# Later chains of squarings: one product and VectorE transposes per step, and the steps dealt out anew

## The chip, the cores and the metric

The kernel runs on one core of a Trainium2 chip. The metric is the device time of one execution in microseconds (us), the median of several runs. TensorE (PE) multiplies matrices, VectorE (DVE), ScalarE (ACT) and GpSimd (POOL) do the element-wise work, and SyncE (SP) issues most DMAs.

## The reference

Four layers are applied to x of 8 batches, 512 channels and 32 x 32 places. The change lies in layer 0, whose core is

```
z = jnp.einsum('bcn,bcm->bnm', f_x, g_x)
S = jnp.linalg.svd(z, compute_uv=False)
sigma = S[:, 0][:, None, None]
attn = z / sigma
z2 = jnp.einsum('bnm,bcm->bcn', attn, h_x).reshape(b, MID, h, w)
return conv1x1(z2, Wv, bv) + x
```

with 64 channels in the middle (MID). Layer 1 is attention over the 1024 places with softmax, with group normalization ahead of it; layer 2 is a second attention with 128 channels; layer 3 is a convolution with the signs of its weights and of its input. Each adds its input. Layers 1 to 3 carry most of the arithmetic.

## The kernel before

**Sigma without a decomposition.** The largest singular value of z squared is the largest eigenvalue of F G, where F and G are the 64 x 64 Gram matrices of f and g. The kernel squares this product again and again and takes traces on the way; sigma comes from the logarithms of the traces. Two batches make a pair: their 64 x 64 matrices stand as two diagonal blocks in a 128 x 128 tile (zero elsewhere), so one matmul squares both. There are four pairs. `gm[j]` holds F, G and the product H of h and g for pair j, each 128 x 128, masked by `mask2` where `gram` (L1337 to L1352) evicts them.

**A chain** (`chain`, from L1016) is the work of one pair: a generator that yields after each of its 22 steps. A matmul gives lhsT transposed times rhs, so squaring a matrix takes its transpose as the stationary operand. The kernel before carries both: `products` (L1026) makes the square (L1029) and the square of the transpose (L1030), each 128 x 128 x 128, and `evict` copies both to SBUF as `cur`, of 128 x 256. Every third step is scaled by the trace of before: a matmul of one column with `mask2` adds up the diagonal (`total`, L1060), VectorE copies it (L1061), takes the reciprocal (L1083) and scales the eviction (L1051). The other two steps are evicted by ScalarE (L1043); on the second of them VectorE takes the diagonal from PSUM (L1056) for the next trace. One chain has 21 steps with a product and 8 totals. The last step writes the scaled H over F (L1112), and `weights0` uses it for the batch.

**The stages.** In an opening, layer 0's projections of all batches, the grams and the weights' products are made. The chain of the first pair in `order` (batches 6 and 7) runs here, with an order of PE's instructions written out by hand, among fillers; it is `chain(jl, True)`, whose two products go to two PSUM banks. The other three chains (`behind`, `chain(j, False)`) run later, between the big products of the batches. The main part has 8 PSUM banks of 128 x 512. It begins with `make_u` for the first batch; then `fast` runs once for each batch: layer 1's scores (`scores1`, 28 yields), v (`make_v`, 14), the values' product (`values1`, 14), layer 2's projections (`project2`), layer 2's scores (`scores2`, 8 tiles) together with the next batch's `make_u`, layer 2's values, and layer 3 (`leave`). The big products follow a scheme of seven products in place of eight (`seven`, matmuls at L388), with evictions by ScalarE, VectorE and GpSimd; values' products stand at L557.

**Where chain steps stand.** `next(behind)` does one step. In `make_u` one is done at every second yield. In `fast` the function `chore(2)` does one at each second call: in `scores1`, where `rest3` (the rest of layer 3 of the batch before) is done and some yields are left out, in `make_v` and in `values1`. There are 66 steps, and in the profile the last product is at 717 us, in the third batch. `entering` (for the batch after the present one) calls the chain's steps at once where its pair is not ready yet. The framework's scheduler then orders the instructions of each engine, so an engine's order can differ somewhat from the program's.

**What hangs on layer 2's sums.** `inverse_sums` (L829 to L838 and on) adds up the exponentials by a matmul, takes the reciprocal on VectorE (L838), writes it to DRAM and reads it back spread over all partitions by DMA (`rfull`); the values are scaled with it (`att`, L967) ahead of the matmuls of `close2` (L675).

Of the kernel before, what the change touches and what calls it, by code (L numbers as in the profile page):

```python
# [16 lines left out]
P = 128  # L17
# [68 lines left out]
def kernel(  # L86
# [96 lines left out]
        return t.rearrange("p g j -> p (g j)")  # L183

    mask2 = block_ones(MID, 1.0, "mask2")
    gmat = block_ones(GROUP, 1.0 / GROUP, "gmat")

    fold = a1.tile([P, 2, MID], F32, tag="fold", name="fold")
# [54 lines left out]

    r_dram = [dram.tile([4, N // 4], F32, name=f"r_dram{i}") for i in range(2 * B)]
    f_dram = [dram.tile([P, HF], F32, name=f"f_dram{b}") for b in range(B)]
    gm = [keep.tile([P, 3, P], F32, tag=f"gm{j}", name=f"gm{j}") for j in range(NPAIR)]
    sw3 = wpool.tile([P, CC, C // 2], F16, tag="sw3", name="sw3")
    round3 = const.tile([P, 1], F32, tag="round3", name="round3")
    nc.gpsimd.memset(round3, ROUND)
# [36 lines left out]
    def weights0(b):  # L286

        rr = side(b % 2)
        ps = bank()
        mm(out=ps, lhsT=gm[b // 2][rr, 0, :], rhs=wv2[rr, :], start=True, stop=True)  # L290
        t = fpool.tile([P, C], F32, tag="pv", name="pv", bufs=2)
        if b % 2:
            nc.vector.tensor_copy(t, ps)
        else:
            nc.scalar.copy(t, ps)
        return t
# [588 lines left out]
    def fast(env, n, hb, ua):  # L885


        b = order[n]
        xt = resident.pop(b)
        more = n + 1 < B  # L890
        ahead = iter(())
        count = [0]

        def chore(every):
            count[0] += 1
            if count[0] % every == 0:
                next(behind, None)

        es = [None] * NT
        for k, _ in enumerate(scores1(env, hb, ua, es)):  # L900
            if rest3 and k % 2 == 0:
                if next(rest3[0], "end") == "end":
                    rest3.pop()
                    if more and order[n + 1] not in resident:
                        resident[order[n + 1]] = load_x(order[n + 1])
            if n == 0 and k == 2:
                weights["o"] = sums_of(quarters_of(wo, chunks, cols2), [so[:, i] for i in range(3)], True)
            if n == 0 and k == 6:
                tp = quarters_of(sbw["tpg"], chunks, [slice(0, P), slice(P, 2 * P)])
                weights["tp"] = sums_of(tp, [sp[:, i] for i in range(3)], True)  # L910
            if k == 8 and more:
                ahead = entering(n + 1)


            if k in (10, 13, 20, 27):
                next(ahead, None)
            if not rest3 and k not in (13, 14, 15, 20, 21, 22):
                chore(2)
        esum = es.pop()
        vt = env["big"].tile([P, NT, C], F32, tag="uv", name="vt")  # L920
        for k, _ in enumerate(make_v(hb, vt)):
            if k == 3:
                r = inverse_sums(env, esum, n)
            if k == 5:
                next(ahead, None)
            chore(2)
        for _ in ahead:
            pass
        scratch = env["big"].tile([P, 3, N], F32, tag="us", name="scratch")
        got = []  # L930
        steps = iter(())
        for k, _ in enumerate(values1(env, xt, vt, es, r, scratch)):
            chore(2)
            if k == 5 and more:
                nxt = resident[order[n + 1]]
                hb = split_h(env, normal(env, nxt))
        signs = None
        if more:
            steps = make_u(env, hb, got)
        else:  # L940
            signs = unpacked(env)

        def fill(k=1):
            for _ in range(k):
                next(steps, None)

        made = []
        for k, _ in enumerate(project2(env, xt, made)):
            fill(k > 5)
        tt, pt, gt = made  # L950
        es, esum = scores2(env, pt, tt, lambda t: fill(t % 2))
        banks, r = [None, None], None

        def values2(h, ts):
            if banks[h] is None:
                banks[h] = bank()
            for t in ts:
                mm(  # L958
                    out=banks[h],
                    lhsT=gt[:, t, :],  # L960
                    rhs=es[t][:, half(h)],
                    start=t == 0,
                    stop=t == NT - 1,
                )
            if t == NT - 1:
                att = env["small"].tile([P, HF], F32, tag="half_b", name="att")
                nc.vector.tensor_tensor(att, banks[h], r[:, h, :], ALU.mult)  # L967
                return att

        dst = channels(out[b])
        fill()
        values2(0, range(0, 2))
        if more:
            r = inverse_sums(env, esum, B + n)
            values2(0, range(2, NTH))
            att = values2(0, range(NTH, NT))
            values2(1, range(0, NTH))
            close2(xt, att, 0)  # L980
            att = values2(1, range(NTH, NT))
            fill()
            for i, _ in enumerate(leave(env, xt, dst, [0])):
                fill(2 * (i % 2))
            close2(xt, att, 1)
            rest3.append(leave(env, xt, dst, [1], stop=True))
            next(rest3[0])
            fill(2)
            for _ in steps:
                pass  # L990
        else:


            r = inverse_rows(env, esum, B + n)
            att = values2(0, range(2, NT))
            values2(1, range(0, 2))
            close2(xt, att, 0)
            values2(1, range(2, 6))
            before, after = leave(env, xt, dst, [0], signs), leave(env, xt, dst, [1], signs)
            count = count_bad(env)  # L1000
            next(count)
            next(before)
            next(before)
            att = values2(1, range(6, NT))
            next(before)
            close2(xt, att, 1)
            for _ in before:
                pass
            next(after)
            next(count)  # L1010
            for _ in after:
                pass

        return hb, got[0] if more else None

    def chain(j, split):  # L1016

        ff, gg, gh = (gm[j][:, i, :] for i in range(3))  # L1020
        tr = spin.tile([P, NSTEP + 3], F32, tag="tr", name="tr")

        def column(name):
            return spin.tile([P, 1], F32, tag=name, name=name)

        def products(a, at):  # L1026
            ps = [bank()] if not split else [bank(), bank()]
            pa, pb = ps[0][:, 0:P], ps[-1][:, 0:P] if split else ps[0][:, P : 2 * P]
            mm(out=pa, lhsT=at, rhs=a, start=True, stop=True)  # L1029
            mm(out=pb, lhsT=a, rhs=at, start=True, stop=True)  # L1030
            return ps[0], pa, pb

        def evict(got, r=None, again=None, full=None):

            both, pa, pb = got
            cur = spin.tile([P, 2, P], F32, tag="cur", name="cur")
            parts = [(cur[:, 0], pa), (cur[:, 1], pb)]
            if not split:
                parts = [(cur.rearrange("p i c -> p (i c)"), both[:, 0 : 2 * P])]
            for i, (dst, ps) in enumerate(parts):  # L1040
                if r is None:
                    if i or not split:
                        nc.scalar.copy(dst, ps)  # L1043
                    else:
                        nc.vector.tensor_copy(dst, ps)
# [6 lines left out]
            return cur  # L1052

        def diagonal(u, v, t):
            d = spin.tile([P, P], F32, tag="diag", name="diag", bufs=1)
            nc.vector.scalar_tensor_tensor(d, u, 1.0, v, ALU.mult, ALU.mult, accum_out=t)  # L1056

        def total(t, s, n=1):
# [19 lines left out]
        for s in range(NSTEP + 1):  # L1078
            got = products(cur[:, 0], cur[:, 1])
            if s:  # L1080
                total(t, s)
                r = column("r")
                nc.vector.reciprocal(r, tr[:, s : s + 1])  # L1083
                if split:
                    r2 = column("r2")
                    nc.vector.tensor_tensor(r2, r, r, ALU.mult)
                cur = evict(got, r, r, r2 if split else None)
            else:
                cur = evict(got)
            yield  # L1090
# [16 lines left out]
        nc.vector.tensor_reduce(rsig, ln, AX.X, ALU.add)  # L1107
        nc.scalar.activation(rsig, rsig, AF.Exp, scale=-0.5)
        nc.vector.tensor_tensor(rsig, rsig, root, ALU.mult)
        for i in range(2):  # L1110
            rr = side(i)
            nc.vector.tensor_scalar(  # L1112
                ff[rr, :].rearrange("p (i c) -> p i c", c=MID),
                gh[rr, rr].unsqueeze(1).to_broadcast([MID, 2, MID]),
                rsig[rr, :],
                None,
                ALU.mult,
            )
        ready.add(j)
        yield  # L1120

# [2 lines left out]

    def chains():
        for j in rest:
            yield from chain(j, False)

    behind = chains()
    env = {}  # L1130
# [208 lines left out]
    def gram(j, i, lt, rhs):  # L1339
        ps = wide()  # L1340
        for t in range(NT):
# [6 lines left out]
            )  # L1348
            if t == NT // 2 - 1:
                yield  # L1350
        nc.vector.tensor_tensor(gm[j][:, i, :], ps[:, 0:P], mask2, ALU.mult)
        yield  # L1352

    def turned_pair(j):
# [99 lines left out]
    relus = iter([(2 * j + k, i) for j in rest for i in range(2) for k in range(2)])  # L1454
    with tc.manual_schedule(engines={mybir.EngineType.PE}):
        steps = entering(0)
        for k, _ in enumerate(chain(jl, True)):

            for _ in range(4 if k == 3 * NSTEP + 3 else 2 if k % 3 == 1 or k == 0 else 1):
                next(todo, None)  # L1460
# [18 lines left out]
    with ExitStack() as main:  # L1479
# [6 lines left out]
        hb = split_h(env, normal(env, resident[order[0]], True))  # L1486

        for k, _ in enumerate(make_u(env, hb, got)):
            if k % 2 == 0:
                next(behind)  # L1490
        ua = got[0]
        for n in range(B):
# [172 lines left out]
```

## Time and profile before

| what | value |
| --- | --- |
| median of 3 runs | 1898.24 us (1897.3 to 1898.89) |
| span of the profiled execution | 1896.9 us |
| PE busy | 1878.3 us |
| PEld (weight loads, beside PE) busy | 976.1 us |
| VectorE busy | 1097.5 us |
| ScalarE busy | 511.4 us |
| GpSimd busy | 225.7 us |
| L1029 and L1030 at 128 x 128 in the whole run | 168 passes each |
| L1051, 128 x 256 | 18 times, 542 ns mean |

The profile comes from one execution; its span runs from the first to the last instruction, and what lies around it is in the runs' times alone. "Busy" counts an engine's own instructions. A matmul of fp32 data shows as two passes, so a count of 2 is one matmul of the program. PE's durations are those of a pipeline: two neighbours overlap, and the distance from start to start is what a matmul takes of PE's time. The granted clock of PE is 0.998 of full speed over the run. The groups carry the line of the kernel, the operation, its output and inputs by the program's names and their shapes; an idle time is followed by what ended it.

### The profile page before, as it was taken

To read this page: it belongs to the slowest core of one execution; us is meant where nothing else is said; L and a number is where in the kernel's file an instruction comes from. 1 tells how busy PE (TensorE), PEld (TensorE's weight loads), DVE (VectorE), ACT (ScalarE), POOL (GpSimd) and SP (SyncE) were. 2 spreads that over 40 slices of the span, in tenths; PEclk is the share of its full clock that TensorE was granted. 3 is DMA by queue.
4 is the path that set the end of the run, shared out by engine and by line. 5 is a ranking of instruction groups with operands and counts; after the bars stand their busy time and mean duration, and the time that the engine had idled before them with its cause. 6 is when DMAs were issued, how large, how long until landed. Compare 5 with 4: busy or idle time off the path is not lost.

```text
span 1896.9 us, 16376 instructions
## 1 busy us (share of the span) xinstructions
PE 1878.3 (99%) x6178; PEld 976.1 (51%) x6178; DVE 1097.5 (58%) x1762; ACT 511.4 (27%) x811; POOL 225.7 (12%) x176
## 2 busy tenths in 40 slices
PE   9999999999999999999999999999999999999997
PEld 3366556544745446444645446544645455544653
DVE  3256576448664677338663675457753775466547
ACT  2142222034312432035202421144202521234013
POOL 0000111201121011200121001200130011101121
PEclk9999999999999999999999999999999999999999
DMA  8420000002000020002000110002000200000001
GB/s 314 168 78 6 1 6 12 1 12 89 17 1 0 34 72 12 1 12 89 18 0 0 42 65 12 0 23 78 12 1 12 89 12 0 1 34 22 12 0 47
DMA packets 25203, 66.52 MB, mean 35 GB/s; under 512 B 3552, under 2 KB 4764, under 8 KB 24476
## 3 DMA queue, kind: packets, MB, share of 16 engines
q1 hardware_dynamic: 24188, 64.96, 9.4%
q8 instruction: 51, 0.84, 0.2%
q10 hardware_dynamic: 864, 0.43, 0.1%
q14 instruction: 36, 0.29, 0.0%
q0 software_dynamic: 64, 0.00, 0.0%
HBM read 46.44 MB, written 18.94 MB: 34 GB/s over the span
## 4 chain that ended last, share of the span: by engine, by line
PE 98%; DVE 1%; ACT 0%; DMA 0%; issue 0%; POOL 0%; ACTq 0%; DVEq 0%
PE bank L388 46%; PE bank L557 20%; PE bank L958 6%; PE bank L806 6%; PE bank L1248 5%; PE bank L658 3%; PE bank L675 3%; PE bank L412 2%; PE bank L698 1%; PE wide L1288 1%; PE bank L1029 1%; PE wide L1342 1%; PE bank L1030 1%; PE quad L1142 1%; PE bank L829 0%; PE bank L1060 0%
## 5 line engine op out<-in xcount | busy, mean ns | idle before, releaser
L557 PE MATMUL bank<-e,vt 128*128 128x512 f32 x768 | 333.8, 592 | 0.0
L557 PEld LDWEIGHTS bank<-e,vt 128*128 128x128 f32 x768 | 145.0, 190 | 175.4 <-issue 173.4
L388 PE MATMUL bank<-ut,h 128*128 128x512 f32 x384 | 182.3, 597 | 0.0
L345 DVE TENSOR_TENSOR e<-bank,e 128x512 f32<-128x512 f32 x128 | 87.8, 686 | 81.0 <-PE bank L388 80.3
L388 PE MATMUL bank<-us,hs 128*128 128x512 f32 x256 | 121.5, 597 | 0.3 <-DVE us L317 0.3
L388 PEld LDWEIGHTS bank<-ut,h 128*128 128x128 f32 x384 | 71.4, 190 | 95.6 <-issue 84.5
L958 PE MATMUL bank<-e,tpg 128*128 128x512 f32 x256 | 114.7, 595 | 0.0
L806 PE MATMUL bank<-tpg 128*128 128x512 f32 x256 | 114.6, 592 | 0.0
L813 ACT ACTIVATE e<-bank 128x512 f32<-128x512 f32 x128 | 76.4, 597 | 128.5 <-PE bank L806 128.5
L360 POOL TENSOR_TENSOR e<-e 128x512 f32<-128x512 f32 x32 | 44.2, 1381 | 412.5 <-ACT e L339 144.1
L388 PE MATMUL bank<-wo,h 128*128 128x256 f32 x384 | 91.9, 382 | 0.0
L388 PE MATMUL bank<-h,wu 128*128 128x512 f32 x192 | 90.4, 593 | 0.1
L818 DVE TENSOR_TENSOR esum<-esum,e 128x1024 f32<-128x1024 f32 x48 | 58.8, 1225 | 54.5 <-ACT e L813 54.5
L345 DVE TENSOR_TENSOR vt<-bank,vt 128x512 f32<-128x512 f32 x64 | 44.1, 689 | 65.5 <-PE bank L388 64.7
L806 PEld LDWEIGHTS bank<-tpg 128*128 128x128 f32 x256 | 48.6, 190 | 60.7 <-issue 60.5
L958 PEld LDWEIGHTS bank<-e,tpg 128*128 128x128 f32 x256 | 48.1, 190 | 60.4 <-issue 60.3
L388 PEld LDWEIGHTS bank<-wo,h 128*128 128x128 f32 x384 | 71.6, 190 | 11.5 <-issue 2.5
L360 POOL TENSOR_TENSOR ut<-ut 128x512 f32<-128x512 f32 x16 | 21.8, 1365 | 465.3 <-ACT ut L341 465.3
L388 PEld LDWEIGHTS bank<-us,hs 128*128 128x128 f32 x256 | 47.1, 190 | 52.9 <-issue 47.8
L686 ACT ACTIVATE sg<-xt,rb 128x512 f16<-128x512 f32 x64 | 45.3, 718 | 100.7 <-DVE xt L677 97.1
L1248 PE MATMUL bank<-xt,fg 128*64 128x512 f32 x256 | 59.9, 616 | 4.4 <-DMA fg<-in_w_fg 4.4
L658 PEld LDWEIGHTS bank<-tpg,xt 128*128 128x128 f32 x512 | 59.5, 192 | 7.2 <-issue 7.2
(333 smaller groups left out, 2968.1 us busy)
## 6 DMA issues: line engine op xcount, KB each, us to landing
xt<-in_x SPq DMA_DIRECT2D x55, 512.0 KB
out<-both SPq DMA_DIRECT2D x63, 256.0 KB
rfull<-r_dram SPq DMA_DIRECT2D x15, 512.0 KB
f_dram<-f SPq DMA_DIRECT2D x8, 256.0 KB
fb<-f_dram SPq DMA_DIRECT2D x8, 256.0 KB
w<-in_w SPq DMA_DIRECT2D x1, 1024.0 KB
q<-in_w_q SPq DMA_DIRECT2D x1, 1024.0 KB
k<-in_w_k SPq DMA_DIRECT2D x1, 1024.0 KB
```

What stands on the lines that cost most here:

```text
L345: nc.vector.tensor_tensor(dst, ps, u, ALU.add)
L360: nc.gpsimd.tensor_tensor(c22, c22, c12, ALU.add)
L388: mm(out=ps[:, q * w : (q + 1) * w], lhsT=lt(ka, kb, q, k), rhs=rhs(ka, kb, q, k), start=first and q == 0 and k == 0, stop=last and k == 1 ...
L557: mm(out=ps, lhsT=a[:, t, bass.ts(r_, P)], rhs=e[t], start=first and t == 0, stop=last and t == NTH - 1, skip_group_check=True,)
L658: mm(out=ps[:, i, :], lhsT=xt[:, cc, bass.ts(4 * h + i, P)], rhs=sbw["tpg"][:, cc, 2 * P : 3 * P], start=cc == 0, stop=cc == CC - 1,)
L675: mm(out=ps, lhsT=sbw["z"][:, bass.ts(oc, P)], rhs=att, start=True, stop=True)
L686: nc.scalar.activation(sg[:, cc, :], xt[:, cc, half(h)], AF.Sign, bias=rb3[:, cc : cc + 1])
L806: mm(out=ps, lhsT=pt[:, 0, bass.ts(t, P)], rhs=tt[:, 0, half(h)], start=True, stop=True,)
L813: nc.scalar.activation(e[:, half(h)], ps, AF.Exp, scale=float(P) ** -0.5)
L818: nc.vector.tensor_tensor(esum, esum, e, ALU.add)
L958: mm(out=banks[h], lhsT=gt[:, t, :], rhs=es[t][:, half(h)], start=t == 0, stop=t == NT - 1,)
L1248: mm(out=banks[i][side(h), :], lhsT=w0[i][:, cc, :], rhs=xt[:, cc, half(h)], start=cc == 0, stop=cc == CC - 1,)
```

## The change

It has three parts.

- **The later chains' step.** `chain` keeps one copy of the matrix as 128 x 64, the two blocks one above the other (`cur`), and the transpose as blocks on the diagonal of `ff`. A step makes one product of 64 columns. `evict` takes 128 x 64 from PSUM, by ScalarE or scaled by VectorE, and `turned` writes its transpose into `ff` by six VectorE instructions: two of 64 x 64, which turn each 32 x 32 block in place, and four of 32 x 32 for the blocks that have to change places. Traces use `eye2`, two identities of 64 one above the other, and diagonals take 64 columns.
- **The tiles.** G and H are kept as 128 x 64 (`gs_`, `gh_`), evicted by two copies of 64 x 64 in place of one masked product; the first pair has a full G, `gg_full`. The first chain is a function of its own, `first_chain`, and keeps its two products; its last scaling is one instruction in place of two.
- **The steps' places.** `chore` now takes a condition: 5 steps in `make_u` of the first batch, 5 in the first batch's `scores1`, and in each batch 4 in `make_v`, 5 in `values1` and 4 in `scores2`.

```
-        def chore(every):
-            count[0] += 1
-            if count[0] % every == 0:
+
+        def chore(now):
+            if now:
                 next(behind, None)
...
-            if not rest3 and k not in (13, 14, 15, 20, 21, 22):
-                chore(2)
+            chore(n == 0 and k in (1, 5, 9, 17, 24))
...
-            chore(2)
+            chore(k in (1, 7, 10, 13))
...
-            chore(2)
+            chore(k in (2, 7, 9, 11, 13))
...
-        es, esum = scores2(env, pt, tt, lambda t: fill(t % 2))
+        def between(t):
+            fill(t % 2)
+            chore(t in (1, 3, 5, 7))
+
+        es, esum = scores2(env, pt, tt, between)
...
+        def product(a):
+            ps = bank()[:, 0:MID]
+            mm(out=ps, lhsT=ff, rhs=a, start=True, stop=True)
+            return ps
+
+        def turned(cur):
+
+            q = MID // 2
+            for i in range(2):
+                nc.vector.transpose(ff[side(i), side(i)], cur[side(i), :])
+            for i in range(2):
+                for k in range(2):
+                    to = slice(i * MID + k * q, i * MID + (k + 1) * q)
+                    of = slice(i * MID + (1 - k) * q, i * MID + (2 - k) * q)
+                    nc.vector.transpose(ff[to, of], cur[of, k * q : (k + 1) * q])
+
+        def evict(ps, r=None, again=None):
+
+            cur = spin.tile([P, MID], F32, tag="cur", name="cur")
+            if r is None:
+                nc.scalar.copy(cur, ps)
+            elif again is None:
+                nc.vector.tensor_scalar(cur, ps, r, None, ALU.mult)
+            else:
+                nc.vector.tensor_scalar(cur, ps, r, again, ALU.mult, ALU.mult)
+            turned(cur)
+            return cur
...
+            for more in range(2 if s < NSTEP else 1):
+                got = product(cur)
+                cur = evict(got)
+                if more:
+                    t = column("tj")
+                    diagonal(got, eye2, t)
+                yield
...
-        nc.vector.tensor_tensor(gm[j][:, i, :], ps[:, 0:P], mask2, ALU.mult)
+        if i == 0 or (i == 1 and j == jl):
+            nc.vector.tensor_tensor((gm[j], gg_full)[i], ps[:, 0:P], mask2, ALU.mult)
+        else:
+            for k in range(2):
+                nc.vector.tensor_copy((gs_, gh_)[i - 1][j][side(k), :], ps[side(k), side(k)])
...
-            if k % 2 == 0:
+            if k in (1, 4, 7, 10, 13):
                 next(behind)
```

More of the change, by code (lines that the diff above doesn't have):

```diff
@@ L185 @@
     mask2 = block_ones(MID, 1.0, "mask2")
+    eye2 = const.tile([P, MID], F32, tag="eye2", name="eye2")
+    nc.vector.tensor_tensor(eye2, ident[:, 0:MID], ident[:, MID:P], ALU.add)
     gmat = block_ones(GROUP, 1.0 / GROUP, "gmat")
@@ L245 @@
     f_dram = [dram.tile([P, HF], F32, name=f"f_dram{b}") for b in range(B)]
-    gm = [keep.tile([P, 3, P], F32, tag=f"gm{j}", name=f"gm{j}") for j in range(NPAIR)]
+    gm = [keep.tile([P, P], F32, tag=f"gm{j}", name=f"gm{j}") for j in range(NPAIR)]
+    gs_, gh_ = (
+        [keep.tile([P, MID], F32, tag=f"{n}{j}", name=f"{n}{j}") for j in range(NPAIR)]
+        for n in ("gg", "gh")
+    )
+    gg_full = keep.tile([P, P], F32, tag="gg_full", name="gg_full")
     sw3 = wpool.tile([P, CC, C // 2], F16, tag="sw3", name="sw3")
@@ L289, in weights0 @@
         ps = bank()
-        mm(out=ps, lhsT=gm[b // 2][rr, 0, :], rhs=wv2[rr, :], start=True, stop=True)
+        mm(out=ps, lhsT=gm[b // 2][rr, :], rhs=wv2[rr, :], start=True, stop=True)
         t = fpool.tile([P, C], F32, tag="pv", name="pv", bufs=2)
@@ L891, in fast @@
         ahead = iter(())
-        count = [0]
-        def chore(every):
-            count[0] += 1
-            if count[0] % every == 0:
+        def chore(now):
+            if now:
                 next(behind, None)
@@ L1014, in fast, with chain, column, diagonal @@
         return hb, got[0] if more else None
-    def chain(j, split):
-        ff, gg, gh = (gm[j][:, i, :] for i in range(3))
+    def chain(j):
+        ff, gg, gh = gm[j], gs_[j], gh_[j]
+        tr = spin.tile([P, NSTEP + 3], F32, tag="tr", name="tr")
+        def column(name):
+            return spin.tile([P, 1], F32, tag=name, name=name)
+        def product(a):
[21 more added lines that the diff above has]
+            return cur
+        def diagonal(u, v, t):
+            d = spin.tile([P, MID], F32, tag="diag", name="diag", bufs=1)
+            for i in range(2) if u is ff else [None]:
+                rr = slice(0, P) if i is None else side(i)
+                uu = u[rr, :] if i is None else u[rr, rr]
+                nc.vector.scalar_tensor_tensor(
+                    d[rr, :], uu, 1.0, v[rr, :], ALU.mult, ALU.mult, accum_out=t[rr, :]
+                )
+        def total(t, s, n=1):
+            ps = bank()
+            mm(out=ps[:, 0:n], lhsT=mask2, rhs=t, start=True, stop=True)
+            nc.vector.tensor_copy(tr[:, s : s + n], ps[:, 0:n])
+        t = column("tj")
+        diagonal(ff, gg, t)
+        got = product(gg)
+        total(t, 0)
+        r = column("r")
+        nc.vector.reciprocal(r, tr[:, 0:1])
+        cur = evict(got, r)
+        yield
+        root, half_ = column("root"), column("half_")
+        nc.gpsimd.tensor_tensor(root, tr[:, 0:1], minus_half[:, 0:1], ALU.pow)
+        nc.vector.tensor_tensor(half_, root, root, ALU.mult)
+        nc.vector.tensor_tensor(half_, half_, tr[:, 0:1], ALU.mult)
+        nc.vector.tensor_scalar(half_, half_, -0.5, 1.5, ALU.mult, ALU.add)
+        nc.vector.tensor_tensor(root, root, half_, ALU.mult)
+        for s in range(NSTEP + 1):
+            got = product(cur)
+            if s:
+                total(t, s)
+                r = column("r")
+                nc.vector.reciprocal(r, tr[:, s : s + 1])
+                cur = evict(got, r, r)
+            else:
+                cur = evict(got)
+            yield
+            for more in range(2 if s < NSTEP else 1):
+                got = product(cur)
+                cur = evict(got)
+                if more:
+                    t = column("tj")
+                    diagonal(got, eye2, t)
+                yield
+        t = spin.tile([P, 2], F32, tag="td", name="td")
+        diagonal(cur, eye2, t[:, 0:1])
+        diagonal(ff, cur, t[:, 1:2])
+        total(t, NSTEP + 1, 2)
+        ln = spin.tile([P, NSTEP + 2], F32, tag="ln", name="ln")
+        rsig = column("rsig")
+        nc.scalar.activation(ln, tr[:, 1:], AF.Ln)
+        nc.vector.tensor_tensor(ln, ln, shares, ALU.mult)
+        nc.vector.tensor_reduce(rsig, ln, AX.X, ALU.add)
+        nc.scalar.activation(rsig, rsig, AF.Exp, scale=-0.5)
+        nc.vector.tensor_tensor(rsig, rsig, root, ALU.mult)
+        nc.vector.tensor_scalar(
+            ff.rearrange("p (i c) -> p i c", c=MID),
+            gh.unsqueeze(1).to_broadcast([P, 2, MID]),
+            rsig,
+            None,
+            ALU.mult,
+        )
+        ready.add(j)
+        yield
@@ L1021, in chain, with first_chain @@
+    def first_chain(j):
+        ff, gg, gh = gm[j], gg_full, gh_[j]
         tr = spin.tile([P, NSTEP + 3], F32, tag="tr", name="tr")
@@ L1026, in products @@
         def products(a, at):
-            ps = [bank()] if not split else [bank(), bank()]
-            pa, pb = ps[0][:, 0:P], ps[-1][:, 0:P] if split else ps[0][:, P : 2 * P]
+            pa, pb = (bank()[:, 0:P] for _ in range(2))
             mm(out=pa, lhsT=at, rhs=a, start=True, stop=True)
             mm(out=pb, lhsT=a, rhs=at, start=True, stop=True)
-            return ps[0], pa, pb
+            return pa, pb
         def evict(got, r=None, again=None, full=None):
[L1035 to L1040, printed above, removed]
+            cur = spin.tile([P, 2, P], F32, tag="both", name="both")
+            for i, ps in enumerate(got):
+                dst = cur[:, i]
                 if r is None:
-                    if i or not split:
+                    if i:
                         nc.scalar.copy(dst, ps)
@@ L1054, in diagonal @@
         def diagonal(u, v, t):
-            d = spin.tile([P, P], F32, tag="diag", name="diag", bufs=1)
+            d = spin.tile([P, P], F32, tag="diag2", name="diag2", bufs=1)
             nc.vector.scalar_tensor_tensor(d, u, 1.0, v, ALU.mult, ALU.mult, accum_out=t)
@@ L1083, in chain @@
                 nc.vector.reciprocal(r, tr[:, s : s + 1])
[L1084 to L1087, printed above, removed]
+                r2 = column("r2")
+                nc.vector.tensor_tensor(r2, r, r, ALU.mult)
+                cur = evict(got, r, r, r2)
             else:
@@ L1109, in chain @@
         nc.vector.tensor_tensor(rsig, rsig, root, ALU.mult)
[L1110 to L1118, printed above, removed]
+        nc.vector.tensor_scalar(
+            ff.rearrange("p (i c) -> p i c", c=MID),
+            gh.unsqueeze(1).to_broadcast([P, 2, MID]),
+            rsig,
+            None,
+            ALU.mult,
+        )
         ready.add(j)
@@ L1126, in chains @@
         for j in rest:
-            yield from chain(j, False)
+            yield from chain(j)
     behind = chains()
@@ L1350, in gram @@
                 yield
-        nc.vector.tensor_tensor(gm[j][:, i, :], ps[:, 0:P], mask2, ALU.mult)
+        if i == 0 or (i == 1 and j == jl):
+            nc.vector.tensor_tensor((gm[j], gg_full)[i], ps[:, 0:P], mask2, ALU.mult)
+        else:
+            for k in range(2):
+                nc.vector.tensor_copy((gs_, gh_)[i - 1][j][side(k), :], ps[side(k), side(k)])
         yield
@@ L1456 @@
         steps = entering(0)
-        for k, _ in enumerate(chain(jl, True)):
+        for k, _ in enumerate(first_chain(jl)):
             for _ in range(4 if k == 3 * NSTEP + 3 else 2 if k % 3 == 1 or k == 0 else 1):
```

## The prediction

> **What bounds the kernel now.** First the page's busy shares (engine, busy us, share of the span, instructions) and its chain of waits.
>
> ```profile
> span 1896.9 us, 16376 instructions
> PE 1878.3 (99%) x6178; PEld 976.1 (51%) x6178; DVE 1097.5 (58%) x1762; ACT 511.4 (27%) x811; POOL 225.7 (12%) x176
> PE 98%; DVE 1%; ACT 0%; DMA 0%; issue 0%; POOL 0%; ACTq 0%; DVEq 0%
> ```
>
> TensorE (PE) is the bound, and the chain agrees. A share is an average, so I next took the waits of PE alone from 190 us to the end, which is the part where the later chains run (columns: total us, times, longest).
>
> ```profile
> PE bank L388 <- DVE us L317: 0.3, 1, 0.3
> ```
>
> That is the whole answer: one wait of 0.3 us in 1700 us. In this part a microsecond of matmuls taken away is a microsecond of the span, as long as no new wait appears. So two things decide: what the chain's matmuls cost in PE's own time, and whether the changed steps come late. For the first, the timeline of PE around three steps (start us, us, line, shape, count; an fp32 matmul of the program is two passes, so x2 is one):
>
> ```profile
> 264.88 0.38 PE L1029 MATMUL bank<-cur 128*128 128x128 f32 x2
> 265.10 0.39 PE L1030 MATMUL bank<-cur 128*128 128x128 f32 x2
> 265.33 1.88 PE L388 MATMUL bank<-us,hs 128*128 128x512 f32 x4
> 267.05 1.88 PE L388 MATMUL bank<-ut,h 128*128 128x512 f32 x4
> 268.76 0.38 PE L1029 MATMUL bank<-cur 128*128 128x128 f32 x2
> 268.98 0.39 PE L1030 MATMUL bank<-cur 128*128 128x128 f32 x2
> 269.21 0.28 PE L1060 MATMUL bank<-tj,mask 128*128 128x1 f32 x2
> 269.35 1.96 PE L388 MATMUL bank<-us,h 128*128 128x512 f32 x4
> 271.15 0.59 PE L388 MATMUL bank<-ut,hs 128*128 128x512 f32 x1
> ```
>
> Durations overlap, so starts are what to read. From 264.88 to 265.33 a step takes 0.45 us: 0.22 for each 128-wide product. The 128x1 total takes 0.14 (269.21 to 269.35), but the x4 group behind it takes 1.80 instead of 1.72 (269.35 to 271.15, against 265.33 to 267.05): together 0.22. One column costs as much as 128 columns.
>
> [...]
>
> **The change part by part.** *PE, removed.* A later chain has 21 products (1 + 6 x 3 + 2), three chains 63. Each was two matmuls of 128 columns (0.45 us); now it is one of 64 columns. Between rows of 1 column (0.22) and 128 columns (0.22) a 64-column one can only cost 0.22[...]. Saved: 63 x (0.45 - 0.22) = 14.2 us, all on the path. The floor of the cost[...] is half the 128-column one, 0.11, which would save 7 us more; the one-column row excludes most of that. The totals (8 per chain) stay.
>
> *VectorE, added.* 63 x 6 = 378 transposes. [...] Bounds: the smallest VectorE rows here take 0.15 (six: 0.9)[...]. I take 1.2: 76 us in all. Off it go some 5 us, since the scaled evictions (18 at 0.54 us) shrink to an estimate of 0.34 from the rows of 256 columns (0.54) and 128 (0.41). VectorE goes from 1097 to about 1167 us, 62%: not a bound on average. ScalarE's copies shrink from 0.37 (256 columns; 0.25 for 128) to about 0.2. Beside other work; nothing for the end.
>
> *The added wait.* In two of three steps VectorE now waits for ScalarE's copy before it transposes, and the next product waits for the transposes. Queued behind that wait on VectorE are evictions of the big products, so banks come free later; PE has eight. Latency of a step: 0.1 to ScalarE, up to 0.6 behind one exponential, 0.2 copy, up to 1.2 behind one VectorE operation, 1.2 turn, 0.1: about 3.0, at most 3.5 us; a scaled step (total, copy, reciprocal, scaling) is similar. The program's order of instructions gives the cover, in PE work between one product and the next: 2 steps have 3.4 us, 23 have 5.2, 10 have 6.9, all others over 8. So the common step is covered, with 1.7 us to spare; uncovered it would cost PE its latency.
>
> *Steps moved.* Before, steps stood also in the scoring stage of all early batches; now 5 stand in forming u, 5 in the first batch's scores, then 13 per batch. 66 steps end in the fifth batch; chain 0 (22 steps) is complete in the first batch and needed in the scores of the second, the others have more room, so nothing is forced early. Nothing moves on SP's or DMA queues, and GpSimd has the same one power per chain. Two places need care. First, forming u: the first product's scaled eviction has 3.4 us of cover, while VectorE is full until 193 us with the normalized input. It takes total, copy 0.15, reciprocal 0.16, GpSimd's power 0.65, scaling 0.34, turn 1.2, from about 193.4 to 196.1, and PE gets there at about 196.1: 0 to 1 us, I take 0.1. Second, layer 2's sums:
>
> ```profile
> 402.13 0.64 PE L829 MATMUL bank<-esum,ones 128*32 128x256 f32 x8
> 402.70 8.85 PE L958 MATMUL bank<-e,tpg 128*128 128x512 f32 x20
> 411.39 3.60 PE L675 MATMUL bank<-att,z 128*128 128x512 f32 x8
> ```
>
> ```profile
> 402.84 1.76 DVE L838 RECIPROCAL rsum<-bank 128x256 f32<-128x256 f32 x1 [3.23 <-PE bank L829]
> 409.80 0.69 DVE L967 TENSOR_TENSOR att<-bank,rfull 128x512 f32<-128x512 f32 x1 [5.21 <-DMA rfull<-r_dram]
> ```
>
> These are PE's and then VectorE's timeline in the first batch (in brackets the idle time before a row and what ended it). PE's L675 starts 0.9 us after att ends (411.39 - 410.49): the slack of the way reciprocal, DMA (5.2 us), att. A step dealt out behind score tile 7 stands ahead of that reciprocal on VectorE. In a plain batch it is over in time: the last sum starts at 397.72 and takes 1.23, so it ends 3.2 us before L829, and the step then needs 0.75 for u's eviction and 1.9 for itself. In the first batch chain 0 ends and chain 1 starts there: two table loads (1.28 us each before) hold up ScalarE's exponentials by some 2.8 us, and the new chain's scaling waits for GpSimd. The reciprocal comes about 2.5 us late, 1.6 more than the slack. So I add 1.6 us, once.
>
> *At nothing:* eye2, the diagonal blocks kept as 64 columns, two small copies per gram instead of one masked product: VectorE work in the opening, where PE's waits are 0.5 us at most and elsewhere. The covering work is the fillers' matmuls; without it some 0.2 us each, 7 times. The first chain keeps its form.
>
> *Sum.* -14.2 + 0.1 + 1.6 = -12.5 us. The span is 1896.9 us, the median of the runs 1898.24, so 1.3 us lie around the span and stay. 1898.2 - 12.5 = 1885.7.
>
> **The rivals.** *A: the queue on VectorE gives half back.* The reciprocal is late in all four batches that have a full set of steps, 1.7 us each (6.8), and the first turn costs 1: 1898.2 - 14.2 + 7.8 = 1891.8. For it: VectorE is near full between score tiles. Against: 2 us of idle time per pair of tiles before, for a turn of 1.2. *B: no new wait and a slightly cheaper product:* 1898.2 - 14.2 - 1.5 = 1882.5. *C: it doesn't do what it says,* as the weight load of each product, now written at the last moment, lies bare: 63 x 0.19 (one load's row) = 12 us back, 1896. Against it: this needs the turn to end just as PE arrives; the cover says 1.7 us earlier. *D: slower, by late turns.* If a step takes L us, PE loses 23 x (L - 5.2) + 2 x (L - 3.4), and for L = 6.0 that is 18.4 + 5.2 = 23.6: 1898.2 - 14.2 + 23.6 = 1907.6. It decides from L of about 5.6 on, where the loss passes the gain; that needs a turn of some 4 us, three times my estimate[...], or two big operations ahead of each one.
>
> **How the numbers follow.** My forecast 0.72, A 0.14, B 0.07, C 0.03, D 0.04. The range 1882.5 to 1891.5 takes in B and nearly A, and leaves out C, D and what lies beyond. About 0.2% (3.8 us) is what a measurement of this kernel can tell from no change; below 1894.4 is faster: forecast, A, B, 0.93; C is the same, 0.03; D slower, 0.04.
>
> **What would show it.** Right: PE's product rows halve to 126 passes of 128x64 at 0.22 us from start to start per two; PE busy falls by some 14 us; VectorE's transposes sum to 60 to 90 us; PE's waits after 190 us stay under 3 us. Wrong: waits of PE for transposed tiles or for att in many batches (A, D), or a product that takes 0.4 us from start to start (C).

## The result, and the profile after

The changed kernel takes 1886.7 us (median of 4 runs, 1886.64 to 1887.44) against 1898.39 us before in the same session (1897.3 to 1898.89). The ratio is 0.9941, with a 95% interval of 0.9929 to 0.9953: 11.7 us less. The spans of the two profiled executions differ by 12.0 us. Here are the page's span, busy shares (engine, busy us, share, instructions) and chain of waits of the changed kernel:

```profile
span 1884.9 us, 16488 instructions
PE 1864.5 (99%) x6052; PEld 962.1 (51%) x6052; DVE 1169.7 (62%) x2156; ACT 504.2 (27%) x811; POOL 221.7 (12%) x176
PE 97%; DVE 2%; ACT 1%; DMA 0%; issue 0%; POOL 0%; ACTq 0%; DVEq 0%
```

PE's busy time falls by 13.8 us (from 1878.3), a little more than the span, so PE is still the bound and about 2 us come back as waits. VectorE's busy time rises by 72 us, to 62%. PE's waits from 186 us to the end (total us, times, longest), which were one of 0.3 us before:

```profile
PE bank L1034 <- DVE gm L1046: 1.1, 1, 1.1
PE bank L395 <- ACT ut L357: 0.7, 1, 0.7
PE bank L682 <- DVE att L975: 0.5, 1, 0.5
```

Three waits, 2.3 us. What a step costs PE now is read from its timeline around an ordinary step, from start to start:

```profile
206.97 0.33 PE L1034 MATMUL bank<-cur,gm 128*128 128x64 f32 x2
207.14 1.94 PE L395 MATMUL bank<-h,wu 128*128 128x512 f32 x4
208.91 1.88 PE L395 MATMUL bank<-h,su 128*128 128x512 f32 x4
```

From 206.97 to 208.91 there are 1.94 us: a group of 1.72, as everywhere, and 0.22 for the product. Before it was 0.45. The transposes among the groups of instructions (busy us, mean ns of one, then idle time before them):

```profile
L1046 DVE STREAM_TRANSPOSE gm<-cur 32x32 f32<-32x32 f32 x252 | 51.1, 203 | 4.5
L1041 DVE STREAM_TRANSPOSE gm<-cur 64x64 f32<-64x64 f32 x126 | 29.9, 237 | 19.1 <-ACT cur L1052 16.7
```

They sum to 81.0 us, and one turn takes 1.36 to 1.41 us from its first start to its last end (six durations would be 2 x 0.237 + 4 x 0.203 = 1.29). The scaled eviction takes 343 ns and ScalarE's copy 212, near the estimates of 0.34 and 0.2.

The largest new wait is in the first batch's scores. PE's row there, with the idle time before it in brackets, and then VectorE's timeline ahead of it:

```profile
219.57 0.43 PE L1034 MATMUL bank<-cur,gm 128*128 128x64 f32 x2 [1.12 <-DVE gm L1046]
```

```profile
214.62 1.22 DVE L325 TENSOR_TENSOR ut<-ut 128x1024 f32<-128x1024 f32 x1
215.75 1.22 DVE L326 TENSOR_TENSOR us<-ut,us 128x1024 f32<-128x1024 f32 x1
216.89 0.15 DVE L1072 COPY tr<-bank 128x1 f32<-128x1 f32 x1
...
217.75 0.34 DVE L1056 TENSOR_SCALAR cur<-bank,r 128x64 f32<-128x64 f32 x1
218.12 0.51 DVE L1041 STREAM_TRANSPOSE gm<-cur 64x64 f32<-64x64 f32 x2
218.67 0.85 DVE L1046 STREAM_TRANSPOSE gm<-cur 32x32 f32<-32x32 f32 x4
```

It is a scaled step. The copy of its trace (L1072) needs 0.15 us, but stands behind the sums that `seven` makes of u (L321 to L326; the first began at 211.68). From there VectorE has hardly a gap until the turn ends at 219.52; one eviction of another product (L352, 0.68 us, among the lines left out) comes in between. PE starts at 219.57. The step's own product was at 212.34, so this scaled step took 7.2 us.

### The profile page after: what moved, and what is told of

The parts are those of the page before. It is cut to its first block, busy times and chain, and to the rows that moved or that the text cites. A ratio compares the mean times of both kernels' runs of the same rounds, so it can differ in the third digit from the quotient of the medians.

```text
span 1884.9 us, 16488 instructions
## 1 busy us (share of the span) xinstructions
PE 1864.5 (99%) x6052; PEld 962.1 (51%) x6052; DVE 1169.7 (62%) x2156; ACT 504.2 (27%) x811; POOL 221.7 (12%) x176
## 4 chain that ended last, share of the span: by engine, by line
PE 97%; DVE 2%; ACT 1%; DMA 0%; issue 0%; POOL 0%; ACTq 0%; DVEq 0%
PE bank L395 46%; PE bank L564 20%; PE bank L813 6%; PE bank L966 5%; PE bank L1353 5%; PE bank L665 3%; PE bank L682 3%; PE bank L419 2%; PE bank L705 1%; PE wide L1393 1%; PE wide L1447 1%; PE bank L1034 1%; PE quad L1247 0%; PE bank L836 0%; PE bank L1140 0%
## 5 line engine op out<-in xcount | busy, mean ns | idle before, releaser
L352 DVE TENSOR_TENSOR e<-bank,e 128x512 f32<-128x512 f32 x128 | 87.6, 685 | 80.2 <-PE bank L395 79.1
L352 DVE TENSOR_TENSOR vt<-bank,vt 128x512 f32<-128x512 f32 x64 | 44.0, 688 | 50.4 <-PE bank L395 50.1
```

Of the source, the lines that this page charges most:

```text
L352: nc.vector.tensor_tensor(dst, ps, u, ALU.add)
```

## The experiments

All are compared with the kernel before, whose median in these sessions was 1898.1 us (41 and 25 runs). The changed kernel ran again beside some of them and took 1886.47 us (median of 5, 1886.06 to 1887.12; ratio 0.9938, interval 0.9925 to 0.9952).

**The two halves of the change, each alone.** First the new step, with the changed tiles that go with it, at the places the steps had before:

```
-            chore(n == 0 and k in (1, 5, 9, 17, 24))
+            if not rest3 and k not in (13, 14, 15, 20, 21, 22):
+                chore(2)
...
-            chore(k in (1, 7, 10, 13))
+            chore(2)
...
-            chore(k in (2, 7, 9, 11, 13))
+            chore(2)
...
-        es, esum = scores2(env, pt, tt, between)
+        es, esum = scores2(env, pt, tt, lambda t: fill(t % 2))
...
-            if k in (1, 4, 7, 10, 13):
+            if k % 2 == 0:
```

> The new step (one product, six transposes) at the steps' places of before. Theory (the gain is PE's saved product, the places only give a step of 2.4 to 3.5 us its cover): the 14 us saved stay, but the old places leave some 25 steps with 3.4 us of PE work between products and 4 with 1.7 to 2.6; those are late by up to 2 us each, so 1889 to 1894 us, with PE waiting for transposed tiles. Rival 1 (the places don't matter, the turn is quick): 1886 to 1887.5. Rival 2 (each short step is late by its whole turn): above 1900.

Measured: 1908.86 us (1906.9 to 1909.25), ratio 1.0056 (1.0042 to 1.007). My 1889 to 1894 missed by 15 us; the theory that put it above 1900 came nearer. The new step without the new places is slower than the kernel before. PE's waits from 180 us in this kernel, the largest line:

```profile
PE bank L1034 <- DVE gm L1046: 14.1, 14, 2.5
```

With the others 16.9 us, against 2.3 in the changed kernel. From the first matmul of forming u to the end the profile has 1718.8 us, against 1698.9: 19.9 us more, 14.6 of them in these waits. From start to start a wait is some 0.15 us longer than the view lists it (at the product below 2.16 us and not 2.00, from 226.58, where the group that starts at 224.86 has had its 1.72 us, to 228.74). For the 16 waits more that is another 2.4 us. The remaining 3 us are open. One of the fourteen waits, as PE's row and VectorE's timeline ahead of it:

```profile
228.74 0.41 PE L1034 MATMUL bank<-cur,gm 128*128 128x64 f32 x2 [2.00 <-DVE gm L1046]
```

```profile
223.60 0.68 DVE L321 TENSOR_TENSOR so<-wo 128x512 f32<-128x512 f32 x1
...
226.61 0.68 DVE L326 TENSOR_TENSOR so<-wo,so 128x512 f32<-128x512 f32 x1
227.21 0.50 DVE L1041 STREAM_TRANSPOSE gm<-cur 64x64 f32<-64x64 f32 x2
227.74 0.85 DVE L1046 STREAM_TRANSPOSE gm<-cur 32x32 f32<-32x32 f32 x4
```

The four sums (L321 to L326) hold VectorE's queue for 3.6 us, from 223.60 to the turn's start at 227.21, and the turn stands behind them. ScalarE's copy was done at 224.68, so the turn starts 2.5 us late, and PE waits 2.00 us. This step takes 5.0 us from product to product (223.78 to 228.74). At the old places 25 products follow the one before within 4.3 us, at the new places 2.

The scaled steps lose most. Seven of the fourteen waits, 9.5 of the 14.1 us, stand behind one. Such a step enters VectorE's queue four times (copy of the trace, reciprocal, scaling, turn), and other work can come in before each: the product at 330.69 starts 9.8 us after the one before it and is still 2.34 us late, with three other operations (3.5 us) between the copy and the turn.

Now the opposite half, the old step at the new places, with the edit above made the other way in the kernel before.

> The two products of before, at the new places. Theory: PE's matmuls are those of before, so about 1898 us; new small waits in forming u (0.7 us at most) and none for evicted squares: 1897.5 to 1899.5. Rival (the places themselves give a good part of the gain, by calmer queues): 1890 to 1895.

Measured: 1898.5 us (1897.58 to 1899.47), ratio 1.0002 (0.9993 to 1.001). As expected, the places alone give nothing: there was one wait of 0.3 us to take away. So the parts don't add up. Alone, the new step costs 10.8 us and the places 0.4; together they save 11.6. Given the new step, the places are worth 22 us.

**What a small matmul costs.** In the kernel before, a matmul takes 0.22 us at 1 column and at 128. Each later step gets one more matmul whose output nobody reads, of 8 columns and, in a second kernel, of 128:

```
         def product(a):
-            ps = bank()[:, 0:MID]
+            full = bank()
+            ps = full[:, 0:MID]
+            mm(out=full[:, P : P + 8], lhsT=ff, rhs=a[:, 0:8], start=True, stop=True)
```

> The changed kernel with one more matmul per later step, 8 columns wide, with the same stationary operand, into an unused part of the bank. Theory[...]: 63 x 0.22 = 13.9 us more, 1900.6 us. Rival (a matmul costs by its columns, so 64 columns cost half of 128[...]): 63 x 0.014 = 0.9 us more, 1887.6.

> The changed kernel with one more matmul per later step as in the run with 8 columns, but 128 columns wide. Theory[...]: as with 8 columns, 1900.5 us, within 1.5.[...]

Measured: 1900.52 us with 8 columns (1899.44 to 1901.2; ratio 1.0012, 1.0004 to 1.0021), 1900.59 us with 128, where the right-hand side is `ff` (1899.35 to 1901.38; 1.0013, 1.0006 to 1.0019). Against the changed kernel's 1886.47 and 1886.7 that is 13.8 to 14.1 us for 63 matmuls, 0.22 us each, at 8 columns as at 128. A pass of 512 columns takes 0.43 us from start to start, by which one of 128 is an estimate of 0.11 us. Had such a time been added for each of the 126 passes to what 8 columns cost, the run with 128 would have been some 14 us longer; it is 0.07 us longer. PE's timeline with 8 columns:

```profile
207.27 0.28 PE L1035 MATMUL bank<-cur,gm 128*128 128x8 f32 x2
207.41 0.41 PE L1036 MATMUL bank<-cur,gm 128*128 128x64 f32 x2
207.66 1.94 PE L395 MATMUL bank<-h,wu 128*128 128x512 f32 x4
209.44 1.88 PE L395 MATMUL bank<-h,su 128*128 128x512 f32 x4
```

Between 207.27 and 209.44 lie 2.17 us, a group's 1.72 and 0.45 for two products. At 1, 8, 64 and 128 columns the price is the same 0.22 us, that of the matmul's existence. So a matmul taken away paid in full, and between these widths a narrower one pays nothing.

**The margin of the turn.** `evict` makes its six transposes twice, from the same tile:

```
             turned(cur)
+            turned(cur)
             return cur
```

> The changed kernel with the six transposes of each step done twice: VectorE has some 80 us more, a step takes 1.35 us longer. Theory (most steps have 5.2 us or more of cover and take 2.4 to 3.5): only the places that wait already get later, forming u, the first scores and layer 2's sums in the first batch, each by 1.4, and perhaps sums in three more batches: 1890 to 1896 us. Rival (latency of the step or VectorE's load decides everywhere): 25 steps late by 1.4, 1920 us or more. Second rival (a step is fully hidden): 1887.

Measured: 1895.21 us (1893.65 to 1897.26), ratio 0.9985 (0.9978 to 0.9991), as expected. VectorE is busy for 1254.6 us (+85). PE's two largest waits from 180 us:

```profile
PE bank L682 <- DVE att L975: 3.8, 4, 2.1
PE bank L1034 <- DVE gm L1046: 3.6, 2, 2.6
```

Of 63 products only two wait, although each turn is 1.4 us longer: the wait in the first scores grows from 1.12 to 2.56, and there is one more in forming u, of 1.02. Most of the rest is layer 2's sums, which are now late in all four batches with a full set of steps. All waits listed are 8.6 us, against 2.3. So the common step has over 1.4 us to spare at the new places, and the way over the sums is next to give.

**The known waits taken away.** The steps are put elsewhere in forming u and the first scores, and the first batch has none behind its last score tile:

```
-            chore(n == 0 and k in (1, 5, 9, 17, 24))
+            chore(n == 0 and k in (3, 6, 9, 12, 17, 24))
...
-            chore(t in (1, 3, 5, 7))
+            chore(t in (1, 3, 5) or (t == 7 and n))
...
-            if k in (1, 4, 7, 10, 13):
+            if k in (0, 5, 8, 11):
```

> The changed kernel with the first batch's steps at other places: 4 in forming u (its yields 0, 5, 8, 11), 6 in the first scores (3, 6, 9, 12, 17, 24), none behind score tile 7 of the first batch. Theory (what is left of waits comes from VectorE's long sums standing ahead of a turn and of layer 2's reciprocal): the waits of 0.7, 1.1 and 0.5 us go, 1884 to 1885.5 us. Rival (they only move to the next step): 1886 to 1888.

The changed kernel as it is, beside it:

> The changed kernel once more, on the same chip as the one with other places: 1886.7 us, within 1.

Measured: 1885.03 us (1884.3 to 1885.19), ratio 0.993 (0.9916 to 0.9943), against 1886.47. PE's waits from 186 us:

```profile
PE bank L395 <- DVE us L324: 0.9, 1, 0.9
PE bank L395 <- ACT ut L357: 0.3, 1, 0.3
```

The waits of 1.1 and 0.5 us are gone, and that of 0.7 in forming u is down to 0.3. A gap of 0.9 has opened at the start of the first scores, where PE waits for the sums of u; a chain step and its total stood there in the changed kernel, and the kernel before had its one wait of 0.3 there. That the missing step is why was read from the order alone. 1.4 us is 0.08%: the ranges of the runs don't overlap, the intervals of the ratios do. It is the fastest kernel of this study.

**The first chain in the new form too.** The opening's hand-written order, with `first_chain` replaced:

```
-        for k, _ in enumerate(first_chain(jl)):
+        for k, _ in enumerate(chain(jl)):
```

and its grams evicted as those of the other pairs.

> The changed kernel with the first chain, in the opening, also in the new form (one product and six transposes). Theory (the new step pays only where its latency of 2.3 us and more is covered): PE saves 21 x 0.23 = 4.8 us, but two of three steps have one filler of 1.7 us or less between products, so some 14 steps come 0.7 to 1.5 us late, and VectorE is busy 60% there: 1890 to 1902 us. Rival (saved products count wherever they are): 1882.

Measured: 1912.93 us (1909.52 to 1914.2), ratio 1.0072 (1.0057 to 1.0087). The sign is as expected and the size too small: 1902 was my upper end. PE's timeline in the opening:

```profile
120.19 0.41 PE L1034 MATMUL bank<-cur,gm 128*128 128x64 f32 x2
120.43 1.08 PE L1393 MATMUL wide<-nat_k,nat_q 128*128 128x512 f32 x2
122.41 0.41 PE L1034 MATMUL bank<-cur,gm 128*128 128x64 f32 x2 [0.91 <-DVE gm L1046]
```

A step takes 2.22 us from product to product (120.19 to 122.41), near the 2.3 us of one with nothing ahead on VectorE in the changed kernel (201.60 to 203.92), and the order of the opening has one filler of 1.1 us for it. In the opening PE waits 14.4 us for turned tiles. Most of the rest came from PE's clock, which is 1.00 from 90 to 210 us in the changed kernel (window, its length, PE busy, granted clock, DMA share, GB/s):

```profile
120.00:130.00 10.00, 6.75 (x23) 1.00 0.00 0
130.00:140.00 10.00, 6.38 (x27) 0.98 0.00 1
140.00:150.00 10.00, 9.19 (x40) 0.50 0.01 2
...
170.00:180.00 10.00, 8.98 (x42) 0.50 0.01 2
```

After some 20 us at about 65% busy the clock is at half in whole windows (0.84 and 0.67 in the two left out, 0.80 from 180 to 190). Busy time times the missing share of the clock, from 140 to 190 us, gives an estimate of 14.6 us lost. Waits and clock, less an estimate of 4.8 us for the products saved, are 24.2 us. The main part begins at 213.13 in place of 186.00, 27.1 us later; the 3 us between are not located. The opening loses twice.

## Why the prediction was right, and where it was not

The forecast was -12.5 us; -11.7 was measured by the medians and -12.0 by the spans. The terms, by the spans:

| term | forecast | measured | by |
| --- | --- | --- | --- |
| 63 products | -14.2 | -13.8 to -14.2 | PE busy, starts; 0.22 us per added matmul |
| first turn, forming u | +0.1 | 0.0 | turn ends 195.56, product at 195.97 |
| layer 2's sums, first batch | +1.6 | +0.5 | wait for att |
| turn behind u's sums, first scores | 0 | +1.1 | wait at 219.57 |
| other waits | 0 | +0.4 | 0.7 in forming u, against 0.3 before at the start of the first scores |
| not located | 0 | +1.0 | what is left |
| opening | 0 | -0.8 | scatter |

With the product at -14.2 they sum to -12.0. The opening's term is scatter: of two executions with the opening of before, the main part starts at 185.67 and at 186.78 us, of seven with the new one between 185.48 and 186.51. Of the unlocated 1.0 us some 0.3 lie behind two products: the groups after those at 195.97 and 219.57 start 0.37 and 0.27 later, not 0.17. At the first the group's weight load is held for VectorE until 196.34. At the second the product's own first load starts only with it, at 219.57; at 206.97 it starts 0.43 us ahead, at 206.54. That this is the cause there was not tested apart, and the rest stays open.

**The product** was right by the bound from both sides: rows of 1 and 128 columns, both 0.22. The extra matmuls confirm it as a price in the time of the whole kernel, not only in starts of a trace. What sets the price was not shown. Weight loads would fit it. In the changed kernel a load's row is drawn 0.19 us long, but the product's second load and the first one behind it start 0.11 us apart:

```profile
206.97 0.19 PEld L1034 LDWEIGHTS bank<-cur,gm 128*128 128x128 f32 x1 [0.24 <-issue]
207.08 0.30 PEld L395 LDWEIGHTS bank<-h,wu 128*128 128x128 f32 x2
```

Two such distances, one for each pass, are 0.22 us, and the estimate of 0.11 us for a pass of 128 columns is no longer than one of them. No run changes the width of the stationary operand, so this stays an estimate of mine from these starts.

**The turn** was mis-sized by some 15%, 1.36 to 1.41 us in place of 1.2. The 1.2 was an estimate of mine that no row of before bears out, as none is a transpose; six rows of 0.15 us gave 0.9, and the turn is above that. It cost nothing where it had cover: with the turn doubled, only two of 63 products wait.

**A step's latency of "at most 3.5 us"** was the step of the argument that failed. It allowed one VectorE operation ahead of the turn, and called a scaled step similar. At 219.57 the trace of the scaled step stood behind u's sums, the step took 7.2 us, and 1.1 us were lost that I had not listed. The same sentence misled my expectation for the new step at the old places by 15 us. By the traces of the waits what decides is the step plus everything that VectorE's queue holds each time the step gets there; no run changes that queue alone. An ordinary step is shorter than I thought: the product at 201.60 has its turn done at 203.92, 2.3 us.

**Layer 2's sums** were late by the mechanism named, and less than I said: the reciprocal starts 2.20 us after the sums on PE (396.27, against 394.07) where it was 0.71 before:

```profile
396.27 1.76 DVE L845 RECIPROCAL rsum<-bank 128x256 f32<-128x256 f32 x1
```

That is 1.5 us late and not 2.5, less the slack of 0.9. Taking the one step away took the wait away. That this term was 1.1 too large, and 1.5 of waits were missing, brought the total near by luck.

**The rivals.** A, the late sums in all batches, is not there at a turn of 1.4 us, and it appears at a doubled one (four waits, 3.8 us). B, a cheaper product, is refuted by the 0.22. C, bare weight loads throughout, is refuted by the starts (0.22 us for the product, not 0.4). D, slower by late turns, didn't happen, but its mechanism is real: the new step at the old places and the first chain in the new form both end slower than before. I gave D a chance of 0.04 on the ground that it needs "two big operations ahead of each one"; at the old places the turn for the product at 228.74 had four operations (3.6 us) ahead of it, and that for the product at 330.69 three operations (3.5 us).

## What to carry to other kernels

- Where PE is full, price a small fp32 matmul by its existence (0.22 us here, from 1 to 128 columns, with 128 stationary columns) and not by its width. Work moved from it to another engine paid only where the longer step was covered: the same step saved 11.6 us at the new places and cost 10.8 at the old.
- Add the queue to the latency: the cover that a step needs is its own time plus the longest burst that the other engine's queue can hold at that place, counted again each time the step comes back to that queue. Look for bursts (here the sums of `seven`) and put the steps elsewhere, and do this together with the change of the step, for either half alone showed nothing or a loss.

## What the hardware did that I had not expected

PE's granted clock fell to 0.50 in whole windows of 10 us of the last kernel (140 to 150 and 170 to 180), though the longest wait of PE between 90 and 190 us was 1.9 us. Many short waits, with PE 64 to 68% busy from 120 to 140, went with the drop; in the changed kernel PE is 97% busy in those 20 us and the clock stays at 1.00. So in this case it was no protection that every gap was short. That the busy share is what decides was not tested apart.
